# Graph layers on one core: factors of softmax and RMS through HBM scratch tensors, and probabilities times v for four row tiles in one operation

## The chip, the cores and the metric

The kernel runs on one core of one Trainium2 chip. The metric is the device time of one execution in microseconds (us). A core has TensorE (PE; its weight loads are shown apart as PEld), VectorE (DVE), ScalarE (ACT), GpSimd (POOL) and the sync engine (SP), which issues all DMAs of this kernel. Sixteen DMA engines move the data between HBM and the on-chip memories: SBUF, with 128 partitions, and PSUM, the banks that TensorE writes its results to.

## What is computed

32 independent graphs (images below) of 512 nodes with 256 features pass through four layers. Each layer adds its result to its input and normalises the sum over the features.

```python
def reference(x, adj, ...):          # x 32x512x256, adj 32x512x512
    # layer 0: masked attention, 8 heads of 32
    q, k, v = split_heads(x @ Wq + bq), split_heads(x @ Wk + bk), split_heads(x @ Wv + bv)
    scores = where(adj > 0, q @ k.T / sqrt(32), NEG)
    out = softmax(scores) @ v
    x = layernorm(x + out @ Wo + bo)
    # layer 1
    h = (1 + eps) * x + adj @ x
    x = layernorm(x + relu(h @ W1 + b1) @ W2 + b2)            # hidden 512
    # layer 2
    h = (eps * x + adj @ x) @ W1 + b1                          # hidden 1024
    h = silu(h * rsqrt(mean(h ** 2) + 1e-6) * rms_weight)
    x = layernorm(x + h @ W2 + b2)
    # layer 3: normalised Laplacian
    xn = layernorm_affine(x)
    x = layernorm(x + softplus(xn @ W_self + (xn - A_norm @ xn) @ W_neigh))
    return x
```

## The kernel before

**An order planned ahead.** The kernel doesn't issue instructions as it goes. `graph(b)` describes one image as a list of operations, each with its engine, a cost in nanoseconds, the buffers it reads and writes, and a function that emits it. `Order.emit` (L258) then sorts the operations of all images into one order per engine: each gets a due time, `b * PERIOD` plus a place in its own image plus a shift of its stage from the table `LEAD`, and a list scheduler (`run`, L108) takes on each engine the operation that is due first among those that can start. So several images are in work at once: the attention of one beside the dense layers of the one before and the last layer of the one before that. Every engine then executes its own list strictly in order, and waits at an instruction whose inputs are not there yet. That holds for SP too: a DMA that waits keeps back all DMAs behind it.

**The array's modes.** The scheduler knows three ways of using TensorE's array: "whole" for ordinary products, "row" for the scores (`sc`, L776), where four heads with a contraction of 32 use four row quarters at once, and "col" for probabilities times v (`po_att`, L893), where four heads write four column quarters at once. It counts a cost for each turn from one to another. An f32 product is two instructions in the profile.

**Attention of an image.** For each group `g` of four heads and each of four row tiles `t` (128 queries): TensorE computes the scores, DVE adds the mask and takes the extreme, ACT takes the exponentials and their row sums into `rs`. DVE transposes the tile in 32x32 blocks, four DMAs write it to a scratch tensor `via` in HBM, and one DMA reads it back as `pT`, which completes the transpose. After every second row tile an operation multiplies two tiles of `pT` with `v` into the bank `po` (`po_att`), two such operations a group. The bank is then copied to `oT`.

**The factors of softmax.** `oT` has the nodes along its columns, while the row sums have them along the partitions. `normalise` takes the reciprocals `rv` (128 x 32), and `split` (L906) cuts them into three bf16 parts, whose sum is the f32 value: three casts and two subtractions on DVE. TensorE transposes the parts (`pm_t`, L934), the result is copied to SBUF, and four products a group with a 0/1 matrix `sel_r` (`pr_r`, L963) add the three parts and spread them over the partitions of each head. DVE multiplies `oT` with that bank (L974).

**The factors of RMS.** In layer 2 the hidden tile `gT` has the nodes along its columns as well. ACT squares its eight parts into `sq`, POOL adds them to `ssq`, DVE transposes and reduces to `red`, one small product `pm` (L1281) gathers the sums, DVE makes the means `ms`, POOL the power `rr` (L567). `split` again cuts `rr` (128 x 4) in three, TensorE transposes (`pm_t`), and four products with `sel_t` (`pb`, L1314) spread it. DVE multiplies the eight parts of `gT` by the bank and the weight (L1326), ACT applies Silu in two halves (L1341), and TensorE multiplies with W2 of that layer, the stage "w22" (L991, `po<-w,gT`).

**Other names that come up.** `ph` are the products with the adjacency (L1170), which need `adjT`, a transposed copy of `adj` loaded by four DMAs a layer-0 image (L589) and put right by DVE and ACT, with a diagonal set by L1152. `pa` and `pg` are the first dense products of layers 1 and 2 (L1187), `pz` (L1436) and `pa_l` (L1478) those of layer 3, `po<-wo,oT` and `po<-w,aT` (L991) the output projections of layers 0 and 1. PSUM has four banks for all of these and one set of four for the scores.

Of the kernel before, what the change touches and what calls it, by code (L numbers as in the profile page):

```python
# [22 lines left out]
PERIOD = 65998  # L23
LEAD = {
    "adjT": 17900, "agg1": -34100, "agg2": -112800, "degree": 46800, "diag": 80200,
    "lap": -5300, "ln0": -81400, "ln1": -47100, "ln2": 88600, "ln3": -37200, "load": -92700,
    "move": 7000, "pv": 8000, "pz": 22200, "qk": 5800, "rinv": -8800, "rms": -91800,
    "scores": -5600, "silu": 57000, "softplus": -39900, "v": -32400, "w11": -49700,
    "w12": -36000, "w21": 10500, "w22": -22500, "wo": 21900, "x3T": -21500, "xT": 67600,
# [30 lines left out]
class Order:  # L60
# [12 lines left out]
    TURN_DUE = 500  # L73
    LATE = 0.09
    HASTE = 137
# [207 lines left out]
def kernel(  # L283
# [54 lines left out]

    ident_b = const.tile([P, P], BF16, name="ident_b")
    nc.vector.tensor_copy(ident_b, ident)

    def selector(n, wide, name):

        of = const.tile([P, n], F32, name=f"{name}_of")
        nc.vector.tensor_reduce(
            of, ident[:, 0 : 3 * n].rearrange("p (r x) -> p x r", r=3), axis=AX.X, op=ALU.add
        )
        sel = const.tile([P, n, wide], BF16, name=name)  # L350
        nc.vector.tensor_copy(sel, of.unsqueeze(2).to_broadcast([P, n, wide]))
        return sel

    NX = 2 * NT * HPG
    sel_r = selector(NX, HD, "sel_r")
    sel_t = selector(NT, P, "sel_t")
# [151 lines left out]
    def graph(b):  # L508
# [60 lines left out]
        def small(name, bufs=2, shape=None):  # L569
# [3 lines left out]
        xs = Buf(sb, [P, NT, D], F32, "x_sb", f"x_{b}", 1)  # L573
        ad = Buf(sb, [P, NT, N], F32, "adj_sb", f"adj_{b}", 1)
        op(
            [("SP", 4000 if first else 8100, lambda: load_x(b, xs), {"issue": 1500 if first else 560, "lat": 300})],
            [], [(xs,)],
# [76 lines left out]
        if early:  # L654
            for c in range(DC):
                pt = bank("pt")

                def tr_x(c=c, pt=pt):
                    for t in range(NT):
                        nc.tensor.transpose(  # L660
                            pt[:, t * P : (t + 1) * P], xs[:, t, c * P : (c + 1) * P], ident
                        )

                pe(460, tr_x, [(xs,)], [(pt,), ("begun", c)], xT)
                evacuate(lambda c=c: xT[:, c, :], pt, [(pt,)], [(xT, c)])
        else:
# [13 lines left out]
        y = tmp([P, NT, D], "y_att", 2)  # L680
        pool(
            2400,
            lambda: nc.gpsimd.tensor_tensor(y(), xs(), rows(bo_r), ALU.add),
            [(xs,), ("bo",)], [(y, t) for t in range(NT)],
# [4 lines left out]
        kT = tmp([P, DC, N], "kT", 2)  # L689
# [3 lines left out]
        def qk(m):  # L693
            stage[0] = "qk"
            for w, w_k, dst, bias_c, bias_k, scale in (
# [16 lines left out]
                to = lambda dst=dst: dst[:, m, :]  # L712
                src = pq
                if dst is kT and not early:
                    to = lambda: kT[:, m, :].rearrange("p (a c s) -> p c a s", a=4, c=4)
                    src = lambda pq=pq: pq().rearrange("p (c a s) -> p c a s", a=4, c=4)
# [45 lines left out]
        def attend(g):  # L762
# [5 lines left out]
            for t in range(NT):  # L768
# [4 lines left out]
                def mm(t=t, sc=sc):  # L773
                    for j in range(HPG):
# [4 lines left out]
                            rhs=kT[hp, g, :],  # L779
# [5 lines left out]
                    870, mm, [(qT, g), (kT, g)], [(sc, j) for j in range(HPG)], mx,  # L785
# [39 lines left out]
                pT = tmp([P, 4, HPG, NT, 32], "pT", 3)  # L825
# [21 lines left out]
                else:  # L847
# [10 lines left out]
                    via = Buf(dr, [4, 32, 4, HPG * NT * 32], F32, "via", f"via_{b}", 4)  # L858
# [24 lines left out]
                if t % 2 == 0:  # L883
                    continue
                stage[0] = "pv"
                two = [(t - 1, pTs[t - 1]), (t, pT)]

                def pv(two=two):

                    for t, pT, c in [(t, pT, c) for t, pT in two for c in range(NT)]:  # L890
                        for j in range(HPG):
# [4 lines left out]
                                rhs=pT[:, :, j, c, :],  # L896
# [5 lines left out]
                    1780, pv,  # L902
                    [(pT, a) for _, pT in two for a in range(4)] + [(v, c) for c in range(NT)],
# [687 lines left out]
```

## Time and profile before

| what | value |
|---|---|
| median of 3 runs | 3356.13 us (3354.51 to 3359.38) |
| profiled execution, its time | 3356.19 us |
| profiled execution, span of the core | 3354.4 us |
| mean granted TensorE clock | 0.996 |
| DMA, share of 16 engines over the span | 76.5%, 767920 packets |

The groups that the change touches, from the list of groups (busy in all, mean of one):

| line | engine, operation | count | busy us | mean ns |
|---|---|---|---|---|
| L893 | PE `po_att<-pT,v` | 8192 | 251.2 | 275 |
| L963 | PE `pr_r<-mT_sums,sel_r` | 256 | 19.8 | 219 |
| L1314 | PE `pb<-mT_rms,sel_t` | 128 | 12.5 | 217 |
| L934 | PE `pm_t`, sums and RMS | 32 + 32 | 7.1 + 7.1 | 221 |
| L1326 | DVE `gT<-gT,rw_c,pb` | 256 | 171.1 | 743 |
| L974 | DVE `oT<-pr_r,oT` | 64 | 43.8 | 686 |
| L850 | DVE transpose of `pq` | 248 | 567.9 | 2296 |

The span is the time from the first to the last instruction of the core. Busy times are unions: products of TensorE overlap, so a mean times a count is more than the busy time. An engine that is busy all the time sets the end; idle time of another engine costs nothing by itself. In the lines of single instructions the columns are start, duration, engine, line, operation, output and inputs, shapes and count, and in brackets the idle time of the engine before it with what ended it.

### The profile page before, as it was taken

The page shows a single profiled execution, that of the slowest core. Times are in us where ns is not written, and L with a number is a line of the kernel's source. Part 1 is how long each engine was busy: PE and PEld are TensorE (multiplying, and loading weights), DVE is VectorE, ACT ScalarE, POOL GpSimd, SP SyncE. Part 2 cuts the span into 40 slices and gives each one's busy share as a digit, 9 for nine tenths or more (in the row PEclk, how much of TensorE's full clock was granted, in tenths as well). Part 3 has the DMA queues.
Part 4 walks back from the last instruction along what each step waited for, and adds up shares of the span by engine and source line. Part 5 has one row for each costly group of instructions (what it writes and reads, how often), then busy time and mean ns, then how long its engine had stood idle before and what let it go on. Part 6 is the DMA issues. An engine that isn't in the chain of part 4 may idle for free.

```text
span 3354.4 us, 55143 instructions
## 1 busy us (share of the span) xinstructions
PE 3305.2 (99%) x19624; PEld 1980.2 (59%) x19624; DVE 2823.6 (84%) x6412; ACT 1887.3 (56%) x3863; POOL 843.4 (25%) x610
## 2 busy tenths in 40 slices
PE   8999999999999999999999999999999999999997
PEld 5556655566565566565666655665655665556654
DVE  7878888888888888888888888888888888888855
ACT  6555565565655655655555655555656556556533
POOL 1222222322222322222222223222222222232221
PEclk9999999999999999999999999999999999999999
DMA  5878878778878787787787787787887887877820
GB/s 143 246 235 216 207 200 222 226 202 211 204 202 234 204 220 197 206 219 226 201 215 207 202 228 214 208 210 201 215 232 199 214 206 201 225 224 183 206 53 13
DMA packets 768195, 677.23 MB, mean 202 GB/s; under 512 B 540208, under 2 KB 592304, under 8 KB 736176
## 3 DMA queue, kind: packets, MB, share of 16 engines
q1 hardware_dynamic: 767920, 673.71, 76.5%
q8 instruction: 155, 2.54, 0.3%
q14 instruction: 120, 0.98, 0.1%
HBM read 380.52 MB, written 293.08 MB: 201 GB/s over the span
## 4 chain that ended last, share of the span: by engine, by line
PE 96%; DVE 1%; ACT 1%; DMA 1%; issue 0%; POOL 0%; SPq 0%; POOLq 0%; DVEq 0%; ACTq 0%
PE po L991 23%; PE ph L1170 13%; PE pg L1187 13%; PE sc L776 8%; PE po_att L893 7%; PE pz L1436 7%; PE pa_l L1478 7%; PE pa L1187 7%; PE pq L703 6%; PE pv L744 3%; ACT pq L814 0%; PE pr_r L963 0%; PE pb L1314 0%; DVE pq L800 0%; DMA via<-pq 0%
## 5 line engine op out<-in xcount | busy, mean ns | idle before, releaser
L814 ACT ACTIVATE pq<-pq,mx 128x512 f32<-128x512 f32 x1024 | 729.0, 714 | 333.3 <-DVE mx L800 265.7
L800 DVE CUSTOM_DVE_ANT_0 pq<-sc,bias 128x512 f32<-128x512 f32 x1024 | 664.3, 685 | 42.3 <-PE sc L776 23.7
L850 DVE STREAM_TRANSPOSE pq<-pq 128x2048 f32<-128x2048 f32 x248 | 567.9, 2296 | 6.4 <-ACT pq L814 6.4
L1187 PE MATMUL pg<-hT,w 128*128 128x512 f32 x1024 | 480.3, 603 | 2.0 <-DVE gT L1242 2.0
L991 PE MATMUL po<-w,gT 128*128 128x256 f32 x2048 | 451.3, 381 | 6.3 <-ACT gT L1341 6.3
L991 PEld LDWEIGHTS po<-w,gT 128*128 128x128 f32 x2048 | 391.3, 191 | 62.1 <-ACT gT L1341 7.1
L549 POOL TENSOR_TENSOR ssq<-ssq,sq 128x512 f32<-128x512 f32 x217 | 276.9, 1276 | 521.6 <-ACT sq L1263 521.2
L1187 PEld LDWEIGHTS pg<-hT,w 128*128 128x128 f32 x1024 | 184.6, 190 | 251.0 <-issue 238.1
L776 PE MATMUL sc<-kT,qT 32*128 32x512 f32 x2048 | 291.9, 640 | 3.0 <-DVE mx L800 3.0
L893 PEld LDWEIGHTS po_att<-pT,v 128*32 128x32 f32 x8192 | 216.3, 110 | 99.1 <-issue 49.2
L893 PE MATMUL po_att<-pT,v 128*32 128x128 f32 x8192 | 251.2, 275 | 5.5 <-DMA pT<-via 5.5
L1478 PE MATMUL pa_l<-zy,adjT 128*128 128x256 f32 x1024 | 243.0, 385 | 0.0
L1044 POOL TENSOR_TENSOR rstd<-ve,nhalf 128x4 f32<-128x4 f32 (+1 forms) x132 | 135.6, 1028 | 422.5 <-DVE ve L1039 417.5
L1242 DVE TENSOR_SCALAR gT<-pg,b_c 128x512 f32<-128x512 f32 x187 | 140.3, 751 | 120.0 <-PE pg L1187 119.9
L549 POOL TENSOR_TENSOR sp<-sp,y 128x1024 f32<-128x1024 f32 x31 | 73.4, 2367 | 657.7 <-ACT sp L1528 644.7
L1436 PE MATMUL pz<-wsn,xnT 128*128 128x512 f32 x512 | 236.9, 606 | 0.7 <-ACT sq L1263 0.6
L1170 PE MATMUL ph<-adjT,y 128*128 128x512 f32 x512 | 227.0, 596 | 4.7 <-ACT y L1070 4.7
L1170 PE MATMUL ph<-adjT,y_att 128*128 128x512 f32 x512 | 228.2, 598 | 0.0
L1187 PE MATMUL pa<-hT,w 128*128 128x512 f32 x512 | 228.1, 598 | 0.0
L991 PE MATMUL po<-w,aT 128*128 128x256 f32 x1024 | 226.5, 379 | 0.0
L991 PEld LDWEIGHTS po<-w,aT 128*128 128x128 f32 x1024 | 194.3, 190 | 28.0 <-ACT aT L1218 0.8
L1478 PEld LDWEIGHTS pa_l<-zy,adjT 128*128 128x128 f32 x1024 | 189.3, 190 | 29.9 <-issue 0.7
(165 smaller groups left out, 4896.3 us busy)
## 6 DMA issues: line engine op xcount, KB each, us to landing
via<-pq SPq DMA_DIRECT2D x992, 256.0 KB, 4.4
pT<-via SPq DMA_DIRECT2D x248, 1024.0 KB, 6.4
adj<-in_adj_dram SPq DMA_DIRECT2D x32, 1024.0 KB, 7.9
adjT<-in_adj_dram SPq DMA_DIRECT2D x124, 256.0 KB, 6.0
x<-in_x_dram SPq DMA_DIRECT2D x32, 512.0 KB, 6.1
xT<-in_x_dram SPq DMA_DIRECT2D x124, 128.0 KB, 5.9
x3d<-y SPq DMA_DIRECT2D x31, 512.0 KB, 3.9
xnT<-x3d SPq DMA_DIRECT2D x124, 128.0 KB, 3.7
```

The source lines that it names most:

```text
L549: lambda: nc.gpsimd.tensor_tensor(dst(), dst(), src(), ALU.add), {},
L703: nc.tensor.matmul(pq(), lhsT=w[:, c, m * P : (m + 1) * P], rhs=xT[:, c, :], start=(c == 0), stop=(c == DC - 1),)
L776: nc.tensor.matmul(sc[:, j, :], lhsT=qT[hp, g, t * P : (t + 1) * P], rhs=kT[hp, g, :], start=True, stop=True,)
L800: lambda t=t, j=j, sc=sc, row=row: nc.vector.tensor_tensor_reduce(out=row(), in0=sc[:, j, :].rearrange("p (a n) -> p a n", a=4), in1=bias[ ...
L814: lambda t=t, j=j, row=row: nc.scalar.activation(row(), row(), AF.Exp, bias=mx[:, t, j : j + 1], scale=-1.0, accum_out=rs[:, g, t, j : j + 1],
L850: lambda pq=pq: nc.vector.transpose(pq().rearrange("p a j c s -> p (a j c s)"), pq().rearrange("p a j c s -> p (a j c s)"),),
L893: nc.tensor.matmul(po[j * HD : (j + 1) * HD, t * P : (t + 1) * P], lhsT=v[:, c, h * HD : (h + 1) * HD], rhs=pT[:, :, j, c, :], start=(c == 0),
L991: nc.tensor.matmul(po[:, i * D : (i + 1) * D], lhsT=lhs[:, k, t * P : (t + 1) * P], rhs=w[:, k, :], start=(i == 0 and k == 0), stop=(i == ...
L1170: nc.tensor.matmul(ph(), lhsT=xin[:, m, c * P : (c + 1) * P], rhs=adjT[:, m, :], start=(m == 0), stop=(m == NT - 1),)
L1187: nc.tensor.matmul(pa(), lhsT=w[:, c, m * P : (m + 1) * P], rhs=hT[:, c, :], start=(c == 0), stop=(c == DC - 1),)
L1436: nc.tensor.matmul(pz(), lhsT=xnT[:, c, t * P : (t + 1) * P], rhs=wsn[:, c, :], start=(c == 0), stop=(c == DC - 1),)
L1478: nc.tensor.matmul(pa[:, i * D : (i + 1) * D], lhsT=adjT[:, m, t * P : (t + 1) * P], rhs=zy[:, m, D : 2 * D], start=(m == 0), stop=(m == N ...
```

## The change

The change does five things.

- **Softmax factors.** `split`, its transposes, the selector matrices and `pr_r` are gone. DVE takes the reciprocals and transposes them in 32x32 blocks; four DMAs write them to a scratch tensor `rd` in HBM, laid out so that a row holds one head's factors of a row tile; four more read them back, each row repeated over the 32 partitions of its head, into `of` in SBUF. The multiply of `oT` reads `of`.
- **RMS factors.** One DMA writes the 512 values of `rr` to `rrd` in HBM in node order, four bytes a piece; one reads them back repeated over all 128 partitions into `pb`, now a tile in SBUF, which shares the one buffer of `sq` (two before).
- **One product operation a group.** `po_att` is emitted once a group of heads, for all four row tiles, when the fourth tile's exponentials are under way in the list. `pT` has four buffers (three before), `via` eight (four).
- **Room.** `x` is loaded straight into `y_att`, and the bias is added there in place; the tile `x_sb` is gone. `kT` is two tiles, one a group, from three buffers of half the size. Two new dependences order the buffers of `y`.
- **The planner's numbers.** `PERIOD`, the table `LEAD`, `TURN_DUE`, `LATE` and `HASTE` have other values, so the order on every engine differs in all stages.

```diff
-PERIOD = 65998
+PERIOD = 62728
 LEAD = {
...
-    TURN_DUE = 500
-    LATE = 0.09
-    HASTE = 137
+    TURN_DUE = 0
+    LATE = 0.31
+    HASTE = -2328
...
-        xs = Buf(sb, [P, NT, D], F32, "x_sb", f"x_{b}", 1)
+        y = tmp([P, NT, D], "y_att", 2)
...
-            lambda: nc.gpsimd.tensor_tensor(y(), xs(), rows(bo_r), ALU.add),
-            [(xs,), ("bo",)], [(y, t) for t in range(NT)],
+            lambda: nc.gpsimd.tensor_tensor(y(), y(), rows(bo_r), ALU.add),
+            [("bo",)], [(y, t) for t in range(NT)],
...
-        kT = tmp([P, DC, N], "kT", 2)
+        kTs = [tmp([P, N], "kT", 3, f"kT{g}") for g in range(DC)]
...
-                pT = tmp([P, 4, HPG, NT, 32], "pT", 3)
+                pT = tmp([P, 4, HPG, NT, 32], "pT", 4)
...
-                    via = Buf(dr, [4, 32, 4, HPG * NT * 32], F32, "via", f"via_{b}", 4)
+                    via = Buf(dr, [4, 32, 4, HPG * NT * 32], F32, "via", f"via_{b}", 8)
...
-                if t % 2 == 0:
+                if t < NT - 1:
                     continue
                 stage[0] = "pv"
-                two = [(t - 1, pTs[t - 1]), (t, pT)]
-
-                def pv(two=two):
-
-                    for t, pT, c in [(t, pT, c) for t, pT in two for c in range(NT)]:
+
+                def pv():
+
+                    for t, c in [(t, c) for t in range(NT) for c in range(NT)]:
...
-                                rhs=pT[:, :, j, c, :],
+                                rhs=pTs[t][:, :, j, c, :],
...
-                    1780, pv,
-                    [(pT, a) for _, pT in two for a in range(4)] + [(v, c) for c in range(NT)],
+                    3500, pv,
+                    [(pT, a) for pT in pTs for a in range(4)] + [(v, c) for c in range(NT)],
...
-        def split(src, n, name):
...
         def normalise():
+
             stage[0] = "rinv"
             rv = small("rv", 2, [P, NX])
+
+            def turned():
+                nc.vector.reciprocal(rv(), rs().rearrange("p g t j -> p (g t j)"))
+                nc.vector.transpose(rv(), rv())
+
...
-            mT = split(rv, NX, "sums")
+            rd = Buf(dr, [NX, P], F32, "rd", f"rd_{b}", 2)
+            of = tmp([P, 2, NT, P], "of", 1)
+
+            def away():
+                for i in range(4):
+                    nc.sync.dma_start(
+                        rd[:, 32 * i : 32 * i + 32], rv[32 * i : 32 * i + 32, :]
+                    )
+
+            def back():
+                v = rd().rearrange("(gt j) q -> j gt q", j=HPG)
+                for j in range(HPG):
+                    nc.sync.dma_start(
+                        of[j * HD : (j + 1) * HD].rearrange("p g t q -> p (g t) q"),
+                        v[j].partition_broadcast(HD),
+                    )
...
-                    lambda g=g, pr_r=pr_r: nc.vector.tensor_tensor(
-                        oT[:, g, :], pr_r(), oT[:, g, :], ALU.mult
-                    ),
-                    [(pr_r,)], [(oT, g)],
+                    lambda g=g: nc.vector.tensor_tensor(
+                        oT[:, g, :], of[:, g].rearrange("p t q -> p (t q)"), oT[:, g, :], ALU.mult
+                    ),
+                    [(of,)], [(oT, g)], port=True,
...
-                sq = tmp([P, N], "sq", 2)
+                sq = tmp([P, N], "sq", 1)
...
-        mT = split(rr, NT, "rms")
-        pb = bank("pb")
...
-        pe(240, spread_rms, [(mT,)], [(pb,)])
+        rrd = Buf(dr, [NT, P], F32, "rrd", f"rrd_{b}", 2)
+        pb = tmp([P, N], "sq", 1, "pb")
+
+        def rr_away():
+            with nc.allow_non_contiguous_dma(reason="one factor per node"):
+                nc.sync.dma_start(rrd().rearrange("t p -> p t"), rr())
+
+        op([("SP", 3000, rr_away, {"issue": 560, "lat": 300})], [(rr,)], [(rrd,)])
+        op(
+            [(
+                "SP", 4500,
+                lambda: nc.sync.dma_start(
+                    pb(), rrd().rearrange("t p -> (t p)").partition_broadcast(P)
+                ),
+                {"issue": 560, "lat": 300},
+            )],
+            [(rrd,)], [(pb,)],
+        )
```

## The prediction

> **What bounds the kernel now.** I read the page first, then the busy time by stretches, then TensorE's instructions in order of time over one image, then the other engines over the same stretch, then the DMA issues. The page:
>
> ```profile
> PE 3305.2 (99%) x19624; PEld 1980.2 (59%) x19624; DVE 2823.6 (84%) x6412; ACT 1887.3 (56%) x3863; POOL 843.4 (25%) x610
> PE   8999999999999999999999999999999999999997
> DMA  5878878778878787787787787787887887877820
> ```
>
> The second and third rows are busy tenths in 40 slices. TensorE idles for 3354.4 - 3305.2 = 49 us, all of it at the two ends. A stretch from the middle (busy us of PE, PEld, DVE, ACT, POOL, then granted clock, DMA share, GB/s):
>
> ```profile
> 1500.00:1600.00 100.00, 100.00 (x600) 59.24 (x599) 85.96 (x196) 57.34 (x120) 26.61 (x19) 1.00 0.80 212
> ```
>
> So in the middle every TensorE nanosecond is on the path, and nothing else is. One image recurs every 102.1 us (the score group `sc` that follows `pr_r` starts at 1455.67 and again at 1557.80). Its TensorE work, as start, duration, instructions:
>
> ```profile
> 1476.81 1.95 PE L893 MATMUL po_att<-pT,v 128*32 128x128 f32 x64
> 1478.69 5.42 PE L1436 MATMUL pz<-wsn,xnT 128*128 128x512 f32 x12
> 1483.94 0.29 PE L1281 MATMUL pm<-red,quad 128*128 128x16 f32 x2
> ...
> 1488.02 1.89 PE L1478 MATMUL pa_l<-zy,adjT 128*128 128x256 f32 x8
> 1489.84 0.22 PE L934 MATMUL pm_t<-ident_b,rmsp 128*12 128x128 bf16 x1
> 1489.99 1.99 PE L1478 MATMUL pa_l<-zy,adjT 128*128 128x256 f32 x8
> 1491.91 0.39 PE L1314 MATMUL pb<-mT_rms,sel_t 12*128 12x128 bf16 x4
> 1492.23 3.72 PE L1478 MATMUL pa_l<-zy,adjT 128*128 128x256 f32 x16
> 1495.89 1.14 PE L776 MATMUL sc<-kT,qT 32*128 32x512 f32 x8
> ...
> 1499.65 13.98 PE L991 MATMUL po<-w,gT 128*128 128x256 f32 x64
> ...
> 1531.62 1.89 PE L744 MATMUL pv<-wv,xT 128*128 128x256 f32 x8
> 1533.35 7.07 PE L991 MATMUL po<-w,aT 128*128 128x256 f32 x32
> ...
> 1555.43 0.22 PE L934 MATMUL pm_t<-ident_b,sumsp 128*96 128x128 bf16 x1
> 1555.49 1.94 PE L1187 MATMUL pg<-hT,w 128*128 128x512 f32 x4
> 1557.26 0.61 PE L963 MATMUL pr_r<-mT_sums,sel_r 96*128 96x128 bf16 x8
> 1557.80 1.14 PE L776 MATMUL sc<-kT,qT 32*128 32x512 f32 x8
> ```
>
> Durations overlap, so costs are start to start: 8 whole-array products of 256 columns take 1533.35 - 1531.62 = 1.73, 216 ns each, and those of 512 columns 429.
>
> **The change, part by part.** *Factors off TensorE.* From 1488.02 to 1495.89 there are 7.87 us. The 32 `pa_l` need 32 x 0.216 = 6.91, and the turn to the row mode of `sc` 0.09 (the eight `pv` ahead of a score group take 1540.25 to 1542.07, 1.82 instead of 1.73), so `pm_t` and `pb` of RMS cost 0.87. The `pr_r` take 0.54, less the same 0.09, which remains: 0.45. The `pm_t` of the sums takes 0.06, and the four `pg` after it 1.77 instead of 1.72: 0.11. Removed: 1.43 us an image, 45.8 us over 32.
>
> *Four row tiles in one operation.* A `po_att` group takes 1.88 start to start (1476.81 to 1478.69) for 16 rounds of four products; inside it a round takes 0.109, so entry and exit cost 0.14. Whole-array work beside it pays too: the twelve `pz` after it take 5.25 instead of 5.15, and work ahead of a turn the 0.09 above. A group between scores and whole-array work adds only the 0.14, since that turn is paid anyway; one between two whole-array stretches adds 0.33. Before, an image has three of the first sort and one of the second: 0.75. In the changed order it has two, each with scores on one side: 0.27. Saved 0.47 an image, 15 us. Products themselves and the number of score turns stay. With the first and last image built in other orders I take 60 us for both savings together, 1.9 an image.
>
> *What goes through HBM instead.* Ten DMAs more an image on SP: four `rd` out, four `of` back, `rrd` out, `pb` back. SP issues a `via` in 0.69 us, so at most 6.9 us more on a queue that issues for some 53 of 102 us. Their 1792 packets, at the page's mean of 0.765 x 16 x 3354.4 us / 768195 = 53 ns, are 6 us of 16 engines an image; by bytes (0.79 MB at 202/0.765 = 264 GB/s), 3. DMA share goes from 80% to 85-88% of a 100.2 us image: no bound.
>
> ```profile
> via<-pq SPq DMA_DIRECT2D x992, 256.0 KB, 4.4
> pT<-via SPq DMA_DIRECT2D x248, 1024.0 KB, 6.4
> adjT<-in_adj_dram SPq DMA_DIRECT2D x124, 256.0 KB, 6.0
> ```
>
> The latency is what may hurt. In RMS the present chain, in the same image:
>
> ```profile
> 1485.26 1.02 POOL L567 TENSOR_TENSOR rr<-ms,nhalf 128x4 f32<-128x4 f32 x1 [5.51 <-DVE ms L1303]
> 1493.42 5.35 DVE L1326 SCALAR_TENSOR_TENSOR gT<-gT,rw_c,pb 128x512 f32<-128x512 f32 x8
> 1496.17 1.92 ACT L1341 ACTIVATE gT<-gT 128x2048 f32<-128x2048 f32 x1 [0.91 <-DVE gT L1326]
> ```
>
> `rr` is there 2.34 after `pm` starts, and from the first multiply to the end of the first Silu pass 4.7 go by. In the changed order `pm` (one `pz` earlier than now) and the first w22 product have between them: two `pz` 3.44, two scores 2.14, four `po` halves 3.46, `pa_l` 6.91, a double `po_att` 3.64 and 0.5 of turns and `pm`: 20.1 us. That leaves 20.1 - 2.3 - 4.9 (with semaphores) = 12.9 for the two legs. No row shows a leg of 4-byte pieces. The lower end is twice the shortest `via` landing, 2.6 each; the upper twice the longest, 9.9. I take two medians of `via` (its pieces are 2 KB like `pb`'s): 8.8. Hidden, with 4 to spare; at the upper end 19.8 - 12.9 = 6.9 an image show. SP waits in order: behind `rrd`'s wait on POOL stands the fourth `pT`, behind `pb`'s wait stand three `xT`, one `via` and then `adjT`.
>
> Pieces under 512 B are no novelty here: 540,208 of 768,195 packets, with TensorE never waiting for them. [...]
>
> *`adjT` behind it.* With `pm` at 8.2 us after the second `po_att` of an image starts, `rrd` goes at 10.8, lands at about 15, `pb` and three `xT` issue until 21 (the `xT` took 4.4), `via` 2.9, `adjT` 5.3: 29. If the engines keep up it lands at 31; if the 2 MB of `via` and `adjT` start only when `pb` and `xT` are through, at 28, they end 8 later at 264 GB/s and land at 37.6. Two transposes (2.4), the copy's last pass (1.2), the diagonal (1.1) and latencies bring its first use to between 36 and 42.6; TensorE, by the prices above, comes there at 42.2. Bounds: nothing, and 2 us if a landing of 6.0 turns into `adj`'s 7.9. I take the late end, 0.4: 12 us over 31 images.
>
> *`pT`.* Four tiles with four buffers: the next four loads start only as the quarters of the running group free them, the worst place being between an image's second group and the next image's first, 24.7 us from start to start on TensorE. Four `pT` and one `via` at 264 GB/s need 20, plus 1.1 to the first free tile and 1.6 to land: 22.7, and the fourth is used 2.6 later than the first. Hidden with 2 to 4.6 spare; the longest landing (9.9 against 6.4) would show up to 1.5.
>
> *Vector work.* Six casts, four subtractions and two copies of 0.16-0.22 go: 2.1 us. A small transpose (0.08 to 0.70) comes, and the multiplies now read the factor from SBUF: between half of L1521's 1.22 and the present 0.74. Cover: DVE has 14 us idle of 100. One buffer for `sq` makes each Square wait for POOL (0.63 + 1.28): seven take 14 us under 20 of `pg`; cover gone, `pm` is late. `x` loaded into `y_att` and the split of `kT` cost nothing: the loads lie images ahead.
>
> *Ends.* The drain has PE idle of 4.8, 2.7, 1.6 and 4.3 before L991, L1170, L991 and L1379. The new last image meets its first norm with no w22 work to cover it (4.3), normalises straight after `po_att` (1.7), runs `pa` straight after `ph` (0.9), and `pm` straight after `pg` (5.0, as 3288.9 to 3293.9 now), besides 2, 1 and 4.3: 19.2 against 13.4. I add 6; bounds -5 and +12, the fill being unknown.
>
> Sum on the profiled execution (3356.2, which is its span and 1.8; the median of the runs is 3356.1): 3356.2 - 60 + 12 + 6 = 3314 us.
>
> **Rivals.** *Half eaten:* `pT` or `adjT` shows 1 us an image: 3302 + 31 = 3333. For it: the spans above come within 1 us. Against: TensorE waited for `pT` 5.5 us in all. *Slower, the RMS round trip:* each leg as slow as `adj`'s landing of 7.9: 15.8 - 12.9 = 2.9 an image, 90 in all, 3392. It decides from legs of 14.6 together (12.9, and the 54 us left after the ends over 31 images). For it: `rrd` queues behind 1 MB `pT`, `pb` behind another. Against: the median landing of 4.4 for `via`. *Not what it says:* TensorE's saving vanishes because another engine is next: DVE at 86 of 100 us and DMA at 88 exclude it; only a wait of 1.5 to 2.0 an image would give 3349 to 3363.
>
> **Numbers.** Forecast (3293 to 3325) 50%, half eaten (3325 to 3349) 23%, within 0.2%, which is what a measurement of this kernel can tell, 6%, the round trip 21%. Faster 0.73, same 0.06, slower 0.21. Range 3293 to 3370: left out are some 14% above and 4% below.
>
> **What would show it.** No `pm_t`, `pr_r`, `pb` rows on PE; 64 `po_att` groups of 128; images 100.2 to 100.8 us apart. PE idle before L991 `po<-w,gT` released by Silu would mean the round trip; before `po_att` by `pT`, the burst; before `ph` by the diagonal, `adjT`. I am wrong if PE falls below 98% in the middle.

## The result, and the profile after

The changed kernel takes 3607.06 us (median of 4 runs, 3605.77 to 3613.98) against 3355.56 for the kernel before: ratio 1.0751, 95% interval 1.0733 to 1.077. It is 7.5% slower, and the prediction (3314, range to 3370) was wrong.

The page of the kernel after: busy time of the engines, then TensorE and DMA in 40 slices.

```profile
PE 3323.0 (92%) x19176; PEld 2013.0 (56%) x19176; DVE 2815.0 (78%) x6075; ACT 1852.5 (51%) x3842; POOL 849.4 (24%) x610
PE   8898899999999999999999999999999999999997
DMA  7777888778897888887788877788987888877821
```

TensorE has 448 product instructions fewer and is busy longer, 3323.0 us for 3305.2, and now idles 282 us of a span of 3604.7. The slices hide it (a 9 is 90% or more); a stretch of 100 us in the middle shows it, in the columns used before:

```profile
1500.00:1600.00 100.00, 93.24 (x555) 54.89 (x552) 83.89 (x183) 55.14 (x115) 26.89 (x19) 0.97 0.85 212
```

The list of waits (total us, times, longest) names the place:

```profile
PE po L954 <- DVE zy L1456: 190.9, 27, 7.8
...
DVE gT L1293 <- DMA pb<-rrd: 254.5, 32, 10.6
```

The timeline of one image, all engines together (start, duration; in brackets the idle time before it and what ended it):

```profile
1593.10 1.02 POOL L549 TENSOR_TENSOR rr<-ms,nhalf 128x4 f32<-128x4 f32 x1 [4.31 <-DVE ms L1266]
1594.15 0.38 SPq L1277 DMA_DIRECT2D rrd<-rr  x1
1605.80 0.32 SPq L1283 DMA_DIRECT2D pb<-rrd  x1
1613.33 5.39 DVE L1293 SCALAR_TENSOR_TENSOR gT<-gT,rw_c,pb 128x512 f32<-128x512 f32 x8 [8.76 <-DMA pb<-rrd]
1616.10 1.91 ACT L1308 ACTIVATE gT<-gT 128x2048 f32<-128x2048 f32 x1 [13.26 <-DVE gT L1293]
1619.71 1.24 DVE L1456 SCALAR_TENSOR_TENSOR zy<-pa_l,ns_out,zy 128x256 f32<-128x256 f32 x3
1620.31 17.05 PE L954 MATMUL po<-w,gT 128*128 128x256 f32 x64 [7.13 <-DVE zy L1456]
```

The factors are ready at 1594.12 and stored at once; SP can issue the load only at 1605.80, when the store has landed, 11.65 us later. The load takes 7.5 more. Then DVE runs its eight multiplies. Silu's first half is done at 1618.01, but w22 starts only at 1620.31: its `po` needs a PSUM bank (no transfer of this kernel goes to or from PSUM) that `pa_l` still holds, and the `zy` that empties it stands behind the multiplies in DVE's queue: they end at 1618.72, the `zy` starts at 1619.71. TensorE has waited 7.13 us.

It then pays again. Windows of the same stretch (length, busy time of PE, PEld, DVE, ACT, POOL, then the granted clock, DMA share, GB/s):

```profile
1616.00:1620.00 4.00, 0.00 (x0) 0.00 (x0) 3.93 (x10) 3.16 (x2) 0.00 (x0) 0.52 0.95 205
1620.00:1622.00 2.00, 1.69 (x4) 1.46 (x5) 2.00 (x5) 1.68 (x2) 0.00 (x0) 0.50 1.19 150
1622.00:1624.00 2.00, 2.00 (x6) 1.56 (x6) 1.93 (x6) 1.97 (x3) 0.00 (x0) 0.50 1.10 129
1624.00:1626.00 2.00, 2.00 (x7) 1.56 (x6) 2.00 (x8) 1.97 (x3) 1.01 (x1) 0.50 0.90 125
```

After the idle stretch the granted clock is 0.50, here for some 6 us of products, in other images for 3, and the products take twice as long: their starts are 0.43 us apart up to 1626.41 and 0.22 after it, and the 64 of w22 last 17.05 us, 13.98 in the kernel before. (The last product before the stretch ends at 1613.18; the granted clock is 1.00 up to 1616.00 and 0.52 on average from there to 1620.00.) From one `pm` to the next the images are now 109.5 us apart (median of images 4 to 28), where before they were 102.1 and TensorE's own list of work, at the prices of the prediction, is 100.2.

What the DMA engines do meanwhile, in windows of 2 us from the issue of `pT` behind the store (the last two columns are DMA share and GB/s):

```profile
1597.00:1599.00 2.00, 2.00 (x10) 1.55 (x10) 1.59 (x5) 0.85 (x3) 0.00 (x0) 1.00 1.01 300
1599.00:1601.00 2.00, 2.00 (x11) 1.77 (x10) 2.00 (x7) 2.00 (x6) 0.00 (x0) 1.00 0.96 78
1601.00:1603.00 2.00, 2.00 (x11) 1.77 (x10) 1.90 (x1) 1.83 (x3) 0.00 (x0) 1.00 0.80 41
1603.00:1605.00 2.00, 2.00 (x11) 1.75 (x10) 1.08 (x2) 0.00 (x0) 0.00 (x0) 1.00 0.43 29
1605.00:1607.00 2.00, 2.00 (x11) 1.76 (x10) 0.00 (x0) 0.00 (x0) 0.00 (x0) 1.00 0.35 49
1607.00:1609.00 2.00, 2.00 (x20) 0.89 (x22) 0.00 (x0) 0.00 (x0) 0.00 (x0) 1.00 0.92 334
```

For 8 us, with a `pT` of 1 MB and an `xT` in the queue, only 29 to 78 GB/s move. That `pT` lands 13.4 us after its issue and the `xT` 14.4; the medians before were 6.4 and 5.9. So it is not only that 2 KB come late: everything that moves comes late. That became the question for the chip.

### The profile page after: what moved, and what is told of

It reads as the page before. It is cut to its first block, busy times and chain, and to the rows that moved or that the text cites. A ratio compares the mean times of both kernels' runs of the same rounds, so it can differ in the third digit from the quotient of the medians.

```text
span 3604.7 us, 54355 instructions
## 1 busy us (share of the span) xinstructions
PE 3323.0 (92%) x19176; PEld 2013.0 (56%) x19176; DVE 2815.0 (78%) x6075; ACT 1852.5 (51%) x3842; POOL 849.4 (24%) x610
## 4 chain that ended last, share of the span: by engine, by line
PE 69%; DMA 18%; DVE 10%; POOL 1%; SPq 1%; ACT 1%; issue 1%; POOLq 0%; DVEq 0%; ACTq 0%
PE po L954 20%; PE ph L1133 12%; PE pg L1150 11%; DMA rrd<-rr 10%; PE pa L1150 6%; DMA pb<-rrd 6%; PE pq L688 6%; PE sc L761 6%; DVE gT L1293 4%; PE po_att L877 3%; PE pv L729 3%; DVE pq L785 2%; DMA via<-pq 1%; PE pz L1403 1%; POOL rr L549 1%
## 5 line engine op out<-in xcount | busy, mean ns | idle before, releaser
L954 PE MATMUL po<-w,gT 128*128 128x256 f32 x2048 | 517.4, 419 | 220.0 <-DVE zy L1456 190.9
L954 PEld LDWEIGHTS po<-w,gT 128*128 128x128 f32 x2048 | 434.0, 214 | 300.2 <-issue 210.0
L1007 POOL TENSOR_TENSOR rstd<-ve,nhalf 128x4 f32<-128x4 f32 (+1 forms) x132 | 143.0, 1084 | 1591.2 <-DVE ve L1002 1590.7
L1150 PE MATMUL pg<-hT,w 128*128 128x512 f32 x1024 | 469.8, 603 | 0.0
L1293 DVE SCALAR_TENSOR_TENSOR gT<-gT,rw_c,pb 128x512 f32<-128x512 f32 x256 | 172.4, 746 | 254.5 <-DMA pb<-rrd 254.5
L1308 ACT ACTIVATE gT<-gT 128x2048 f32<-128x2048 f32 x64 | 122.3, 1910 | 414.1 <-DVE gT L1293 414.1
L1403 PE MATMUL pz<-wsn,xnT 128*128 128x512 f32 x512 | 245.7, 617 | 0.5 <-DVE mine L1258 0.5
L877 PE MATMUL po_att<-pT,v 128*32 128x128 f32 x8192 | 241.1, 275 | 2.7 <-issue 2.0
L1445 PE MATMUL pa_l<-zy,adjT 128*128 128x256 f32 x1024 | 227.3, 380 | 1.2 <-ACT zy L1430 1.2
```

The source lines that it names most:

```text
L877: nc.tensor.matmul(po[j * HD : (j + 1) * HD, t * P : (t + 1) * P], lhsT=v[:, c, h * HD : (h + 1) * HD], rhs=pTs[t][:, :, j, c, :], start=( ...
L954: nc.tensor.matmul(po[:, i * D : (i + 1) * D], lhsT=lhs[:, k, t * P : (t + 1) * P], rhs=w[:, k, :], start=(i == 0 and k == 0), stop=(i == ...
L1150: nc.tensor.matmul(pa(), lhsT=w[:, c, m * P : (m + 1) * P], rhs=hT[:, c, :], start=(c == 0), stop=(c == DC - 1),)
L1293: lambda m=m: nc.vector.scalar_tensor_tensor(out=gT[:, m, :], in0=gT[:, m, :], scalar=rw_c[:, m : m + 1], in1=pb(), op0=ALU.mult, op1=ALU. ...
L1403: nc.tensor.matmul(pz(), lhsT=xnT[:, c, t * P : (t + 1) * P], rhs=wsn[:, c, :], start=(c == 0), stop=(c == DC - 1),)
L1445: nc.tensor.matmul(pa[:, i * D : (i + 1) * D], lhsT=adjT[:, m, t * P : (t + 1) * P], rhs=zy[:, m, D : 2 * D], start=(m == 0), stop=(m == N ...
```

## The experiments

### Is it the wait, the queue, or the small pieces?

Theory A: the round trip of the RMS factors is late and the rest follows, either because store and load queue behind large transfers on SP (A1) or because the store goes in 512 pieces of four bytes (A2). Rival: something else in the changed order. Four edits of the changed kernel, all in the two RMS transfers (e1_const leaves the factors out of the result):

```diff
 e1_const   (a scratch of ones, written once; rrd is still stored)
-    pb(), rrd().rearrange("t p -> (t p)").partition_broadcast(P)
+    pb(), rrc.rearrange("t p -> (t p)").partition_broadcast(P)
 e2_poolq, e3_actq   (both transfers; .gpsimd in e2, .scalar in e3)
-    nc.sync.dma_start(rrd().rearrange("t p -> p t"), rr())
+    nc.gpsimd.dma_start(rrd().rearrange("t p -> p t"), rr())
 e4_rows   (rr is padded to 128x32; rows of 128 bytes)
-    nc.sync.dma_start(rrd().rearrange("t p -> p t"), rr())
+    nc.vector.transpose(rr(), rr())
+    for i in range(4):
+        nc.sync.dma_start(rrd[:, 32*i : 32*i+32], rr[32*i : 32*i+NT, :])
```

> The changed kernel with the same order, but the RMS factors that are read back come from a scratch tensor written once at the start (all ones), so nothing waits for this image's factors; both DMAs are still issued, and the factors are left out of the result. Theory A (the RMS round trip sets the end): pb is issued some 7 us sooner, the 7 us wait ahead of the w22 products goes, an image takes 100 to 101 us, in all 3300 to 3330 us. Theory B (the softmax round trip, the pT burst or the order as a whole): 3500 us or more.

> The changed kernel with the same order, both RMS DMAs issued by POOL, which is idle there for 30 us, instead of SP. Theory A1 (rrd and pb stand in line behind pT, via and xT of the same queue): both legs together fall from 18.5 to 6 to 10 us, in all 3300 to 3380 us. Theory A2 (512 pieces of 4 bytes are slow in themselves): the first leg stays near 11 us, 3530 us or more.

> The same with ACT issuing both DMAs. A1: legs of 3 to 5 us each, but ACT stands still behind its waits for some 4 us an image, 3330 to 3450 us. A2: first leg near 11 us and ACT blocked as long, over 3600 us.

> The changed kernel with the same order of operations, the RMS factors first transposed in 32x32 blocks on DVE, so that they leave in 16 rows of 128 bytes by four DMAs instead of 512 pieces of 4 bytes by one. A1 (standing in line): the leg stays at 10 to 12 us, 3590 to 3620 us. A2 (the pieces): the leg falls to 3 to 5 us, 3330 to 3420 us.

Measured: e1_const 3574.64 (ratio 1.0651, 1.063 to 1.0671), e2_poolq 3589.86 (1.0696, 1.0678 to 1.0714), e3_actq 3576.82 (one run), e4_rows 3369.0 (one run). e1 is the miss that taught most. Theory A's 3300 to 3330 is far off, and the time lies in the band of its rival, the rest of the order, which e4 then rules out. Nobody waits for the store in e1, and only 32 of the 251 us come back, because `pb` now takes 12.7 us to land (median; 6.9 before that edit) and `xT` 12.0. Another queue gives back 17 or 30 us, so A1 falls; e2 is where A2 put it (3530 or more), e3 below A2's 3600 but far above A1's 3450. Rows of 128 bytes give back 238, inside A2's band: it is the pieces, and they cost more through the other transfers than through the wait for the store itself.

### The store by itself

Is it the number of the pieces, or that they lie side by side? Three edits of e1_const, where `rrd` is not read and the factors are left out of the result, so that only the store is meant to differ:

```diff
 e6_nowrite
-    nc.sync.dma_start(rrd().rearrange("t p -> p t"), rr())
 e7_apart   (rrd is [P, NT, P]: each piece 512 bytes from the next)
-    nc.sync.dma_start(rrd().rearrange("t p -> p t"), rr())
+    nc.sync.dma_start(rrd[:, :, 0:1], rr().unsqueeze(2))
 e8_16b   (rrd is [P, NT])
-    nc.sync.dma_start(rrd().rearrange("t p -> p t"), rr())
+    nc.sync.dma_start(rrd(), rr())
```

> e1_const without the write: pb is read from the constant scratch, nothing is stored to rrd. The RMS factor is left out of the computation. Same order on every engine but for the one DMA. Theory A (the write alone stops the other transfers): 3310 to 3370, some 200 us below e1_const's 3574.6; pb and pT land within 8 us of their issue. Rival B (the transfer of 256 KB to pb, or the order itself, is what costs): within 40 us of e1_const.

> e1_const with the 512 four-byte pieces stored 512 bytes apart, in 256 KB of scratch, where they stood side by side in 2 KB. The RMS factor is left out of the computation. Theory A (it is the number of small pieces): as e1_const, 3550 to 3590. Rival B (it is that neighbours write into the same stretch of memory): as e6_nowrite, 3310 to 3380.

> e1_const with the factors stored partition by partition, 128 pieces of 16 bytes side by side in the same 2 KB. The RMS factor is left out of the computation. Theory A (number of pieces): a quarter of e1_const's loss over e6_nowrite is left, some 50 us, about 3420. Rival B (neighbours in the same stretch): between a quarter and all of it, since as many bytes of each stretch are written from different partitions, 3420 to 3590. A result at e6_nowrite's time would speak against both.

Measured: e6_nowrite 3616.11 (1.0773, 1.0753 to 1.0792), e7_apart 3391.74 (1.0104, 1.0086 to 1.0123), e8_16b 3418.41 (1.0184, 1.0165 to 1.0202). e7 has the instructions, the order, the bytes and the number of pieces of e1; only the addresses differ, and 183 us are gone. So it is the neighbourhood, not the count, although e7 ends 12 us above the 3380 that the rival had as its upper end. e8, side by side but in 128 pieces of 16 bytes, takes 27 us more than e7; that is also what the theory of the count forecast (about 3420), so e8 by itself decides nothing. At which distance between 4 and 512 bytes the cost goes was not measured.

e6 missed both expectations (the rival's by 1.5 us), and could not be read as meant: without the store's operation the planner made another order, in which `pb` is issued right behind three `pT` of 1 MB and lands 11.6 us later behind them, with the DMA engines at a share of 1.01 and at 203 to 418 GB/s (1503 to 1511), not stopped. It is the same wait with another cause, and says nothing of the store. What it did teach is to take out work without touching the planner, which the next two do: a store to a scratch nobody reads, added to the kernel *before*, inside an operation that the planner already has.

```diff
 e9_b_side   (scr is [NT, P])
+    nc.gpsimd.dma_start(scr.rearrange("t p -> p t"), rr())
 e10_b_apart   (scr is [P, NT, P])
+    nc.gpsimd.dma_start(scr[:, :, 0:1], rr().unsqueeze(2))
```

> The kernel before with one transfer more per image and nothing else: as soon as the RMS factors are there, GpSimd's queue stores them as 512 four-byte pieces side by side in 2 KB of a scratch that nobody reads. Every engine's order stays as it was. Theory A (such a store stops the other transfers for 6 to 9 us, wherever it stands): probabilities or x land late and the time rises by 2 us per image or more, 3420 to 3600. Rival B (only the place in the changed kernel's burst makes it costly): 3355 to 3385.

> As e9_b_side, but the 512 four-byte pieces go 512 bytes apart, over 256 KB of unread scratch. Theory A (neighbours in the same stretch of memory are what costs, as e7_apart against e1_const says): 3350 to 3390, far below e9_b_side. Rival B (the number of pieces): within 20 us of e9_b_side.

Measured: e9_b_side 3471.76 (1.0347, 1.0322 to 1.0372), e10_b_apart 3358.34 (1.0003, 0.9994 to 1.0012). Theory A on both counts: the same 512 pieces cost 115 us side by side and nothing that can be measured apart. TensorE meets the cost mostly ahead of `ph`, in a row that the kernel before doesn't have:

```profile
PE ph L1169 <- ACT y_att L1069: 74.8, 29, 4.1
```

Windows of e9_b_side around a store that GpSimd issues at 1533.42, then of e10_b_apart around one at 1487.69:

```profile
1532.00:1534.00 2.00, 2.00 (x12) 0.48 (x10) 1.10 (x4) 0.28 (x1) 1.60 (x2) 1.00 0.99 384
1534.00:1536.00 2.00, 2.00 (x10) 1.77 (x11) 1.90 (x8) 0.55 (x1) 0.22 (x1) 1.00 0.66 158
1536.00:1538.00 2.00, 2.00 (x10) 1.46 (x9) 1.00 (x6) 1.68 (x6) 0.00 (x0) 1.00 0.05 5
1538.00:1540.00 2.00, 2.00 (x12) 1.44 (x11) 1.13 (x4) 0.01 (x1) 0.00 (x0) 1.00 0.00 0
1540.00:1542.00 2.00, 2.00 (x11) 1.74 (x11) 2.00 (x4) 1.98 (x3) 0.00 (x0) 1.00 0.00 0
1542.00:1544.00 2.00, 2.00 (x13) 0.88 (x12) 2.00 (x4) 1.09 (x2) 0.00 (x0) 1.00 0.67 66
```

```profile
1486.00:1488.00 2.00, 2.00 (x11) 0.50 (x9) 1.06 (x6) 0.51 (x1) 1.32 (x2) 1.00 1.02 404
1488.00:1490.00 2.00, 2.00 (x12) 1.63 (x9) 1.90 (x9) 0.31 (x1) 0.43 (x1) 1.00 0.90 271
1490.00:1492.00 2.00, 2.00 (x10) 1.47 (x9) 1.23 (x6) 1.92 (x6) 0.00 (x0) 1.00 0.28 42
1492.00:1494.00 2.00, 2.00 (x13) 1.44 (x12) 0.86 (x2) 0.00 (x0) 0.00 (x0) 1.00 0.83 283
```

Side by side, the 16 engines move almost nothing for 6 us; apart, traffic dips for one window. Part of that emptiness is SP's queue, which is in order. In e9_b_side it stands still for 9 us; in e10_b_apart the same two are issued at 1487.20 and 1490.95:

```profile
1532.92 0.59 SPq L588 DMA_DIRECT2D xT<-in_x_dram  x1
1542.27 0.34 SPq L873 DMA_DIRECT2D pT<-via  x1
```

That `pT` waits for a `via` issued at 1527.8, before the store, which landed only after 14.4 us, and the `xT` took 9.5; apart, the same two take at most 8.6 and 4.4. So what the store holds up in the first place is the landing of transfers that are already under way, and through SP's order all that stands behind them. The view of the tile `scr` has the landing of the store itself, shortest, median and longest, in e9_b_side and in e10_b_apart:

```profile
DMA to landing us min/median/max: 8.4/9.4/11.9
```

```profile
DMA to landing us min/median/max: 2.2/3.5/6.6
```

### What is left: the other two parts

e4_rows is free of the stop and still far from 3314. It was timed again, and one line for the planner was tried on it, since TensorE was late there ahead of `ph`. This was put down to the `adjT` load, which comes last in a burst:

```diff
 e11_rows   (e4_rows unchanged)
 e12_late   (the x loads, on e4_rows)
-    [("begun", c) for c in range(DC)], [(xT, c, q) for c in range(DC)],
+    [("begun", c) for c in range(DC)] + [(adjT, 0, 1)], [(xT, c, q) for c in range(DC)],
```

> The kernel of e4_rows once more, timed in rounds against the kernel before. Both theories: 3362 to 3376, some 0.3% above the kernel before; an interval that reaches below 1 would leave it open.

> The kernel of e4_rows with one line for the planner: the loads of x count as due only after the second quarter of adjT is there. The planner then puts the adjT and x loads of an image earlier in SP's queue, out of the burst of probabilities that ends at the RMS factors; TensorE's list sums to 3231.5 us (3244.0 before that line). Theory A (what e4_rows still loses, 1.4 us per image ahead of ph and pv, is the late adjT load): 3290 to 3340, below the kernel before. Rival B (another order makes another late wait): 3360 or more.

Measured: e11_rows 3377.85 (1.0063, 1.0046 to 1.008), e12_late 5214.42 (1.5534, 1.5511 to 1.5558). e11 ends 2 us above its band; e12 is on the side of its rival. On the chip e11 has images 102.5 us apart for a list of 100.2. Three waits of TensorE make most of the 2.2, each in most of the images (us in total, times, longest):

```profile
PE pv L727 <- PE ph L1131: 17.7, 27, 0.7
PE po L952 <- DVE zy L1462: 15.1, 17, 1.7
PE ph L1131 <- PE po L952: 12.9, 22, 0.6
```

`po` still meets the bank behind the multiplies. The other two rows name TensorE's own work, which was long done, so the trace has to say what was awaited. In the image at 1540, DVE sets the diagonal of `adjT` just ahead of `ph`, and transposes `xT` just ahead of `pv`:

```profile
1539.32 0.69 DVE L1113 TENSOR_TENSOR adjT<-diag,self 128x512 f32<-128x512 f32 x1
1540.21 7.11 PE L1131 MATMUL ph<-adjT,y_att 128*128 128x512 f32 x16 [0.63 <-PE po L952]
1546.64 1.24 DVE L657 STREAM_TRANSPOSE xT<-xT 128x1024 f32<-128x1024 f32 x1
1547.98 3.69 PE L727 MATMUL pv<-wv,xT 128*128 128x256 f32 x16 [0.66 <-PE ph L1131]
```

`pv` starts 0.10 us after that transpose in all 27 waits, `ph` 0.21 us after the diagonal in the 22 of its own. Both stand in DVE's queue behind the RMS multiplies, and from the first multiply (1518.55) to the end of the `xT` transpose (1547.88) DVE pauses for 0.16 us only. The multiplies in turn wait for the factors:

```profile
DVE gT L1299 <- DMA pb<-rrd: 44.8, 27, 6.4
```

No load of `adjT` is late there: DVE waits for one in two images, 4.1 us in all. So what e11 still loses in the middle is again the RMS round trip, by way of DVE's order, and e12's line was aimed at the wrong wait. e12 is the worst run of the study although its list is the shortest: the planner moved `pT` to where `po_att` stands still 124 times.

```profile
PE po_att L875 <- DMA pT<-via: 695.0, 124, 17.5
```

The remaining parts were then run apart (the RMS part alone on the kernel before was not), and two of the mixtures again with the planner's old `PERIOD` and `LEAD` (its other three numbers stayed as changed), to tell the order from the parts:

```diff
 e5_rms_pe   (the changed kernel; split, sel_t and pb of the kernel before)
-    op([("SP", 3000, rr_away, ...)], [(rr,)], [(rrd,)])
+    mT = split(rr, NT, "rms")
+    pe(240, spread_rms, [(mT,)], [(pb,)])
 e13_sums   (the kernel before)
-    mT = split(rv, NX, "sums")
+    op([("SP", 4800, away, ...)], [(rv,)], [(rd,)])
+    op([("SP", 5800, back, ...)], [(rd,)], [(of,)])
 e14_four   (e5_rms_pe, with normalise, sel_r and pr_r of the kernel before)
-    op([("SP", 4800, away, ...)], [(rv,)], [(rd,)])
-    op([("SP", 5800, back, ...)], [(rd,)], [(of,)])
+    mT = split(rv, NX, "sums")
+    pe(240, spread, [(mT,)], [(pr_r,)])
 e15_rms_pe_old, e16_rows_old   (e5_rms_pe and e11_rows, with all of the old LEAD)
-PERIOD = 62728
+PERIOD = 65998
```

> The change with the RMS factors back on TensorE; the softmax factors through HBM and the four-tile products stay. By its list TensorE has 3272.9 us to do (before 3303.2, the whole change 3244.0). Theory A (the RMS write of 512 four-byte pieces is the whole loss): no more stops of the DMA engines, and the time follows TensorE's list, 3325 us (3310 to 3340), below the kernel before. Rival B (what was left over in e4_rows, some 2 us per image ahead of ph, comes from the other two parts): 3370 to 3395, no gain against the kernel before.

> The kernel before, with the softmax factors alone through HBM (128-byte rows), the old planner's numbers, the old products and the RMS factors on TensorE. TensorE's list sums to 3286.6 us, 16.6 below before. Theory A (the terms are as priced, and hidden under an order without late waits): 3335 to 3347. Rival B (the factors' way through HBM brings a wait of its own): 3357 or more.

> The change's products of four row tiles and its planner's numbers alone; both factors stay on TensorE as before. TensorE's list sums to 3289.4 us, 13.8 below before. Theory A (the term as priced): 3335 to 3350. Rival B (the change's order has late waits of its own, the adjT load ahead of ph above all): 3365 to 3420.

> e5_rms_pe with the planner's table of the kernel before (the two constants PERIOD and LEAD), nothing else changed. Its list is steady from image to image (101.1 us each, where e5_rms_pe's goes 98 to 110). Theory A (e5_rms_pe lost by its order, not by its parts): 3315 to 3345, below the kernel before. Rival B (the parts lose): 3400 or more.

> e11_rows with the planner's table of the kernel before. TensorE's list has 100.2 us per image, as e11_rows. Theory A (e11_rows' last 1.5 to 2 us per image are its order's): 3290 to 3345. Rival B (the RMS round trip, with legs of some 7 us each, doesn't fit into the order at all): 3370 or more.

Measured: e5_rms_pe 3571.85 (1.064, 1.0625 to 1.0655), e13_sums 3376.66 (1.0057, 1.0042 to 1.0072), e14_four 3437.36 (1.0238, 1.0223 to 1.0253), e15_rms_pe_old 3661.16 (1.0908, 1.0889 to 1.0928), e16_rows_old 3574.06 (1.0643, 1.0627 to 1.0658). Every expectation of theory A missed. e13, e15 and e16 lie where their rivals put them; e5 and e14 lie above both bands. e5's list goes 98 to 110 us from image to image, and on the chip 94 to 123; but e15, whose list is steady, is slower still: there `ph` waits for `y` and `pa_l` for the multiplies, each once an image, together 6.0 of the 10.8 us by which its images (111.9 us apart) exceed the list (101.1).

```profile
PE ph L1181 <- DVE y L1073: 95.4, 27, 5.8
PE pa_l L1489 <- DVE gT L1337: 67.7, 27, 2.5
```

So a shorter list of TensorE's work gives a shorter time only in an order whose other chains fit it, and neither table of planner numbers makes one for these mixtures. The waits name part of what is late in each order; whether the parts themselves stand in the way was not separated from the order. That some order exists that keeps the gain of all three parts was not shown, and stays open.

e13 alone is steady, and better than its total. Its `pm` of the first images, and of two in the middle:

```profile
157.05 0.37 PE L1293 MATMUL pm<-red,quad 128*128 128x16 f32 x2 [0.49 <-DVE s_in L1129]
282.30 0.40 PE L1293 MATMUL pm<-red,quad 128*128 128x16 f32 x2
398.26 0.29 PE L1293 MATMUL pm<-red,quad 128*128 128x16 f32 x2
499.83 0.29 PE L1293 MATMUL pm<-red,quad 128*128 128x16 f32 x2
...
1515.58 0.29 PE L1293 MATMUL pm<-red,quad 128*128 128x16 f32 x2
1617.15 0.29 PE L1293 MATMUL pm<-red,quad 128*128 128x16 f32 x2
```

From the third on the images are 101.57 us apart, where before they are 102.13: 0.56 less. The first `pm` comes 10.5 us later than before, and the first two intervals are 125 and 116 where before they are 112 and 102: some 38 us lost at the start. Two edits on that start:

```diff
 e17_start   (the planner's keys, on e13_sums)
-    keys[o.n] = b * period + d - ...
+    keys[o.n] = b * period + min(b, 2) * 1000 + d - ...
 e18_first3   (on e13_sums)
+    if b < 3:
+        wide = tmp([P, NX, HD], "of", 1, "wide")
+        nc.vector.tensor_copy(wide(), rv().unsqueeze(2).to_broadcast([P, NX, HD]))
+        ... nc.tensor.transpose(pr_r[...], wide[:, x : x + HPG]..., ident)
```

> e13_sums with one line of the planner changed: images 1 and later are due 1 us, images 2 and later 2 us later than before, which makes the list of the first images nearly that of the kernel before and leaves the order of the later ones as it was in e13_sums. Theory A (e13_sums' first images lose 27 us by their order): 3335 to 3347, below the kernel before. Rival B (the first images lose by the round trip itself): within 8 us of e13_sums' 3376.7.

> e13_sums with the softmax factors of the first three images spread by TensorE (the reciprocals copied wide on VectorE, then eight transposes) and those of the other 29 through HBM; the planner's numbers are those of the kernel before. Theory A (the gain of 0.56 us per image is real and only the start hid it): about 29 x 0.56 = 16 us below the kernel before, 3337 to 3347. Rival B (the start or the end of the list loses again): 3353 or more.

Measured: e17_start 3360.54 (1.0012, 1.0003 to 1.0021), e18_first3 3335.7 (0.9934, 0.9921 to 0.9948). e17 lies between its two expectations: 16 us come back, and some 24 of the 38 stay, 6 ahead of the first `pm` and 18 in the first interval (129.5 us). That the first image has no earlier one beside it to hide the way through HBM is the likely reason; no run shows it apart from the order. In e18, with TensorE spreading the factors of three images, the first `pm` and the first interval are within 3 us of the kernel before, and the gain stays. e18_first3 beats both kernels, by 0.66% and 7.5%, and is 1.3 us below theory A's band. It has the softmax part alone: the RMS factors and the products of two tiles are those of the kernel before. Its page, and a stretch of the middle, where TensorE is busy throughout:

```profile
PE 3288.7 (99%) x19360; PEld 1964.5 (59%) x19360; DVE 2809.4 (84%) x6251; ACT 1874.0 (56%) x3861; POOL 843.4 (25%) x610
```

```profile
1500.00:1700.00 200.00, 200.00 (x1185) 118.31 (x1184) 172.52 (x383) 113.56 (x239) 52.40 (x38) 1.00 0.84 220
```

## Why the prediction was wrong

- **What bounds it.** Right for the kernel before, and the sign to look for was well chosen: PE at 93.24 of 100 us in the middle, below the 98% named. The wait was named at the right instruction, w22's `po`; its releaser is `zy`, not Silu.
- **The failed step: the two legs of the RMS round trip, "I take two medians of `via` (its pieces are 2 KB like `pb`'s): 8.8. Hidden, with 4 to spare".** Measured medians are 11.6 and 6.9 us, 18.5 together. That is inside the upper end stated (19.8), so the bound was sound and the choice in it was not: the row taken has 2 KB pieces, and the leg that mattered has four-byte ones. "Pieces under 512 B are no novelty here" was the wrong comfort: 507,904 of those 540,208 packets are the 128-byte pieces of `adjT`, `xT` and `xnT` (124 issues of each, 256, 128 and 128 KB), all of them loads from HBM. The runs show that the size of a piece does not decide by itself (512 writes of four bytes, 512 bytes apart, cost nothing in e10_b_apart: 3358.34, ratio 1.0003), and that four-byte neighbours do (e9_b_side: 3471.76, 1.0347). Why neighbours do, inside the memory or the engines, no run shows.
- **What that step left out.** It priced the legs as latency of their own. The store stops the other transfers too (29 to 78 GB/s for 8 us in the changed kernel): e1_const, with nobody waiting for it, still loses 219 us.
- **The 12.9 us left for the legs.** Too much by some 2: it counted to the end of Silu's first half (4.9 us with semaphores) where the freed bank counts. From the landing of `pb` (1613.3) to w22 (1620.31) it is 7.0.
- **The restart.** Not in the sum at all. From start to start the w22 products take 15.8 us an image after, 13.9 before: 1.9 us an image at a granted clock of 0.50. With the idle time of about 7 and half a microsecond elsewhere this makes the 9.4 us between 109.6 (the mean of images 6 to 25) and 100.2.
- **Factors off TensorE.** The part for the sums was priced at 0.45 + 0.11 = 0.56 us an image, and e13_sums and e18_first3 show 0.56. The RMS part, 0.87, was in no run a gain in time: e11_rows and e16_rows_old take it off TensorE, and lose it to waits.
- **Four row tiles, 0.47.** On TensorE's rows a part of it is there: e14_four's `po_att` take 7.26 us an image from start to start, those of the kernel before 7.54: 0.28. As time it was not realised: e14_four is 80 us slower than the kernel before, in an order in which `ph` waits most (38.7 us in 20 waits).
- **`adjT` late by 0.4.** Behind the RMS wait it can't be seen after. In e11_rows `ph` waits for the diagonal 12.9 us in all, close to the 12 of the sum, but by luck: the load is there in time, and what makes the diagonal late is DVE's queue behind the multiplies, which wait for `pb`. The same queue delays `xT` ahead of `pv` by 17.7 us, which no term of the sum has.
- **`pT`.** Right: no wait of `po_att` for it shows among the changed kernel's.
- **The ends, +6.** Without the stop (e11_rows against the kernel before) the first `pm` comes 4.8 later and the next three intervals are 9.8 longer, the last two and the drain no longer: 14 where +12 was the upper bound.
- **The rivals.** The slower one had the place right, and that both legs are late; the reason given for it, standing in line behind `pT`, fell with e2_poolq and e7_apart. Its condition (legs of 14.6 together) came true; at its formula 18.5 would have given 18.5 - 12.9 = 5.6 us an image, some 3475. The rest is the bank, the restart and the start. Its chance was put at 21% on the strength of `via`'s median, a row of another kind.

Had the stop been the only error, e11_rows would stand at 3314. It stands 64 us above: 2.2 us an image over the list is 58 for the 26 images in the middle, less the 12 that the sum had for `adjT`; the rest, some 18, lies in the first and last images, which gain nothing of the 1.9 either. A sum of TensorE's work alone was thus a lower bound here; of the mixtures, only e13_sums and e18_first3 kept the whole gain that they were priced at, and only in the middle.

## What to carry to other kernels

Before a store of one element per partition in node order is put on HBM, look at its pieces: transpose on chip and write rows (e4_rows: 3369.0 us, the changed kernel 3607.06), or leave the pieces apart (512 bytes in e7_apart: 3391.74, e1_const 3574.64); four-byte neighbours held up the core's other transfers, not just their own (0 to 78 GB/s for some 8 us). When a value is sent round through HBM, price it to the moment the next bound engine can really start (its bank, the in-order queue that frees it, its clock after an idle stretch, here 0.50 for 3 to 6 us), and treat the first image, which has nothing beside it, on its own. Where a planner orders the work, test a part by adding it inside an operation that the planner already has, since a changed list moves everything.

## What the runs showed of the hardware

- 512 writes of four bytes side by side in 2 KB: 8.4 to 11.9 us to land in e9_b_side, and the core's 16 DMA engines at 0 to 78 GB/s for some 8 us, from either of two queues (0 to 66 in e9_b_side from GpSimd's, 29 to 78 in the changed kernel from SP's). Transfers under way landed late in e9_b_side: a `via` after 14.4 us, an `xT` after 9.5. The same 512 writes 512 bytes apart: 3.5 us (median), and no cost in time (e10_b_apart, ratio 1.0003). 128 writes of 16 bytes side by side: 27 us in all over 512 apart (e8_16b 3418.41, e7_apart 3391.74).
- After about 7 us without a product (the wait ahead of w22, images 6 to 25 of the changed kernel) TensorE was granted clock 0.50 for 3 to 6 us of the work that followed: 1.9 us an image.
